# A two-layer convolution block: stores of the first layer on another queue, and another order of work at the edges of an image

## The chip, the cores and the metric

The kernel runs on one core of a Trainium2 chip. The metric is the device time of one execution in microseconds (us); for the kernel before it is 3935.01 us, the median of three runs (3934.5 to 3936.88). A core has five engines that run side by side, each taking its own instructions in order: TensorE (PE; its weight loads are shown as PEld), VectorE (DVE), ScalarE (ACT), GpSimd (POOL) and SyncE (SP), which here only issues DMA transfers.

## The reference, cut to what matters

x is 8 images of 256 channels and 64 x 64 pixels, in float32. Two residual layers follow one another:

```python
x = x + L0_conv_ref(gn(x), ...)
x = x + L1_conv_ref(gn(x), ...)

# layer 0 (per image): a 3x3 kernel made for every pixel and every group of 8 channels
x1, x2, x3 = conv1x1(x, w1, b1), conv1x1(x, w2, b2), conv1x1(x, w3, b3)
h = relu(bn(concat(x1, unfold3(reflect_pad(x2)))))       # 320 channels
w = conv1x1(relu(bn(conv1x1(h, cw1))), cw2, cb2)          # 9 weights for each of 32 groups
out = einsum('bgskhw,bgkhw->bgshw', unfold3(zero_pad(x3)), w)

# layer 1 (per image): 7x7 local attention (4 heads of 64) and a mix of depthwise convolutions
q, k, v = c1x1(x, Wq, bq) / 8, c1x1(x, Wk, bk), c1x1(x, Wv, bv)
att = softmax(einsum('bdn,bdkn->bnk', q, unfold7(reflect_pad(k)) + unfold7(reflect_pad(pe))))
out_att = einsum('bnk,bdkn->bdn', att, unfold7(reflect_pad(v)))
wts = softmax over 9 branches of einsum('oc,bchw->bohw', Wfc, x)
out_conv = sum over branches of wts * dwconv(relu(dwconv(x, w1)), w2)
out = rate1 * out_att + rate2 * out_conv
```

gn is a group norm with 32 groups, over whole images: layer 1 of an image can't start before layer 0 of that image is done.

## The kernel before, in words

An image is cut into NB = 8 bands of 8 rows (512 pixels); B * NB = 64 bands in all. One loop, `for g in range(-AHEAD, B * NB)` with AHEAD = 12 (L1030), makes layer 1 of band g and, beside it, layer 0 of a band some 12 further on. So in the first 12 turns (g < 0, called `alone`) only layer 0 runs; in the last 12 only layer 1. Every turn has STEPS = 8 steps, s = 0 to 7. The order of instructions on each engine is the order in which the program emits them; nothing reorders them.

Within a step there are fixed slots: `steer(g, s)` first (loads), then layer 1's scores and exponentials, a first `branch_weights` (L868), the functions in the list `mid`, a second `branch_weights`, and last the functions in the list `end`. `beside(g, s)` (L913) fills `mid` and `end`. A counter of places, `advance()`, moves on six times in a step; `after(n, f)` emits f n places later. A turn thus has 48 places: steer of step s is at place 6s, mid at 6s + 2, end at 6s + 5.

**Layer 0 of a band.** `load_x` (L99) brings x by channel (xc for the maps, xs for the statistics of a later image). `small_maps` (L328) makes x1 and x2. `value_maps` (L362) makes x3 in two halves: PE products L369, ScalarE adds the bias into x3n (L374), and SyncE stores x3n to DRAM (L375). In the alone turns this is in mid of steps 2 and 3, places 14 and 20. `x_by_group` (L399, steer of step 4) loads x again in another arrangement, xg: 32 groups x 4 quarters of the band on the 128 partitions, 8 channels x 128 pixels each; four DMAs (L405) of 128 KB, in pieces of 512 bytes. `values_by_group` (L381, step 5) loads x3 from DRAM in the same arrangement (x3q; L389, L393, L397: five DMAs, the last from the next band). `hidden_maps` (L409) has ScalarE make hid(0), hid(1), hid(2) (L420), PE convolve them (L430), and ScalarE write h2n (L437). `tap_weights` (L459) multiplies: PE makes weights pw (L466) from h2n, VectorE multiplies them with x3q into prod (L479), and POOL adds prod into xg (L487). In alone turns there are three groups of three taps; the third product of each goes to PE, which sums in PSUM (`gather`, L500), and VectorE adds that sum into xg (`combine`, L507, place 14 of the next turn). The products of a band are at places

```python
TAPS_AT = (1, 2, 3, 4, 5), (0, 2, 4)
PRODUCTS_AT = ((1, 2),) * 5, ((7, 14, 10), (9, 17, 13), (12, 20, 16))
```

(right-hand sets for alone turns: 12, 19, 15, then 26, 34, 30, then 41, 49, 45; the last of each three goes to PE). Prod has two buffers, so a product waits for the add before last. `take` (L509), one place after the sum, has VectorE make statistics (L515) and SyncE store xg to DRAM as x1 (L519, four DMAs). From turn -1 on the band's nine products all go to POOL.

**Layer 1 of a band.** `load_rows` (L547) loads a band of x1 with three rows on both sides into yp, `normalise` (L559) applies the group norm on ScalarE (L562). `values` (L575) makes v in two halves of two PSUM tiles (PE L592, ScalarE copies L600 into vc, one buffer), `store_values` (L607) writes vc to DRAM with its mirrored columns (L616; then L621, or L625 where the two halves of a row pair hold different numbers of rows), `mirror_rows` (L632) the mirrored rows, and `value_tile` loads the attention's tiles vt (L643). `position` (L650) makes the position map on POOL, `queries` (L661) makes qb (PE pq, ScalarE) and allots kb, with a POOL copy of the last rows of the band before; `keys` (L680) makes kb (PE pk, VectorE L700 and L707, and at the edges mirrored rows on ScalarE, L717). Scores (L736) read qb and kb, masks and maxima are on VectorE (L750), exponentials on ScalarE (L758, L767), transposes on PE (L773), weighted values on PE (L785). `branch_weights` is PE pf (L872) and ScalarE ex (L877). The PSUM tag "gen" (four buffers) holds pf, ptp, pq, pk, pv, pw and p3 in turn.

Edge bands are the first and last of an image. Their key products have other sizes (11 new rows for the first, 5 for the last, 8 inside), and in the last band of an image the next image's first two bands are loaded and two chunks of its values made. In the kernel before, `beside` puts for edge bands: queries of the second channel half at step 1 and its keys at step 2, queries and keys of the next band at steps 5 and 6; for inner bands these are steps 2, 3, 6 and 7. The last, keys of an inner band at step 7, are emitted ahead of `branch_weights` (L1055 to L1059).

Of the kernel before, what the change touches and what calls it, by code (L numbers as in the profile page):

```python
# [18 lines left out]
P = 128  # L19
# [4 lines left out]
R = 8  # L24
# [62 lines left out]
def conv_layers_kernel(ctx: ExitStack, tc: tile.TileContext, ins: dict, out: bass.AP):  # L87
# [271 lines left out]
        if i == NB - 1:  # L359
            nc.gpsimd.tensor_copy(t[0:96, R + 1, :], t[0:96, R - 1, :])  # L360

    def value_maps(b, i, mt):  # L362

        im = images[b]
        if mt == 0:
            im.x3[i] = dram.tile([C, R, HP], F32, tag="x3", name=f"x3_{b}_{i}")
        p3 = ps.tile([P, BAND], F32, tag="gen", name=f"p3_{b}_{i}_{mt}", bufs=4)
        for kt in range(NCT):
            nc.tensor.matmul(  # L369
                p3, im.w3s[:, kt, mt * P : (mt + 1) * P], im.xc[i][:, kt, :],  # L370
                start=(kt == 0), stop=(kt == NCT - 1),
            )
        p3 = p3.rearrange("p (r c) -> p r c", r=R)
        nc.scalar.activation(x3n[mt][:, :, 1 : 1 + W], p3, AF.Identity, bias=im.bias[:, 1 + mt : 2 + mt])  # L374
        nc.sync.dma_start(out=im.x3[i][mt * P : (mt + 1) * P], in_=x3n[mt])  # L375

    def pieces(v, q):

# [20 lines left out]
    def x_by_group(b, i, alone):  # L399

        tag, pool = ("ex", w1) if alone else ("xg", w0)
        t = pool.tile([P, SHARE, SR, W], F32, tag=tag, name=f"xg_{b}_{i}", bufs=3 if alone else 2)
        images[b].xg[i] = t
        for q in range(NQR):
            nc.sync.dma_start(  # L405
                out=t[q * REL : (q + 1) * REL].rearrange("p s r c -> p s (r c)"), in_=pieces(x_in[b][:, i * BAND : (i + 1) * BAND], q)
            )

    def hidden_maps(b, i, alone):  # L409

# [48 lines left out]
    def tap_weights(b, i, u, alone, at):  # L459
# [49 lines left out]
        def take():  # L509
            x = im.xg[i]  # L510
            if i == 0:
                im.st1 = stat.tile([P, 2 * NB, 6], F32, tag="st1", name=f"st1_{b}")
            for t in range(2):
                v = x[:, t * SHARE // 2 : (t + 1) * SHARE // 2].rearrange("p s r c -> p (s r c)")
                nc.vector.bn_stats(im.st1[:, 2 * i + t, :], v)  # L515
            t = im.x1[i] = dram.tile([C, BAND], F32, tag="x1", name=f"x1_{b}_{i}")
            for q in range(NQR):
                v = x[q * REL : (q + 1) * REL].rearrange("p s r c -> p s (r c)")
                nc.sync.dma_start(out=pieces(t, q), in_=v)  # L519

        for j in range(n):
            after(at[j], lambda j=j: product(j))
# [46 lines left out]

    def value_rows(j):  # L570

        first, last = (PAD, R) if j == 0 else (0, R) if j < NB else (R - 1, R + PAD)
        return first, last, first if j < NB else 0

    def values(b, j, half):  # L575

        im = images[b]
        if half == 0:  # L580
            im.vc[j] = w1.tile([P, R // 2, C], F32, tag="vc", name=f"vc_{b}_{j}", bufs=1)
        vc, yp = im.vc[j], im.yp[min(j, NB - 1)]
        first, last, _ = value_rows(j)
        pv = ps.tile([P, 2, C], F32, tag="gen", name=f"pv_{b}_{j}_{half}", bufs=4)
        done = []
        for g in range(2):
            r = first + 4 * half + 2 * g
            n = min(2, last - r) * W
            if n <= 0:
                break  # L590
            for kt in range(NCT):
                nc.tensor.matmul(  # L592
                    pv[:n, g], yp[:, kt, r : r + n // W].rearrange("p r c -> p (r c)"), wv[:, kt],
                    start=(kt == 0), stop=(kt == NCT - 1),
                )
            done.append(n)

        def take():
            if len(set(done)) == 1:
                nc.scalar.copy(vc[: done[0], 2 * half : 2 * half + len(done)], pv[: done[0], : len(done)])  # L600
            else:
                for g, n in enumerate(done):
                    nc.scalar.copy(vc[:n, 2 * half + g], pv[:n, g])

        return take

    def store_values(b, j):  # L607

        im = images[b]
        vc = im.vc[j]  # L610
        vd = im.vd[j] = dram.tile([R, WP, C], F32, tag="v", name=f"vd_{b}_{j}")
        first, last, at = value_rows(j)
        count = [(last - first + 1 - p) // 2 for p in range(2)]
        for p in range(2):
            to = vd[at + p : at + p + 2 * count[p] - 1 : 2, PAD : PAD + W]
            nc.sync.dma_start(out=to.rearrange("u c n -> c u n"), in_=vc[p * W : (p + 1) * W, : count[p]])  # L616
        for d in range(1, PAD + 1):
            for to, c in ((PAD - d, d), (PAD + W - 1 + d, W - 1 - d)):
                if count[0] == count[1]:
                    o = vd[at : at + 2 * count[0], to].rearrange("(u p) n -> p u n", p=2)  # L620
                    nc.sync.dma_start(out=o, in_=vc[c : c + W + 1 : W, : count[0]])  # L621
                else:
                    for p in range(2):
                        o = vd[at + p : at + p + 2 * count[p] - 1 : 2, to : to + 1].rearrange("u c n -> c u n")
                        nc.sync.dma_start(out=o, in_=vc[p * W + c : p * W + c + 1, : count[p]])  # L625

    def mirror_rows(b, j):

# [21 lines left out]
    def position(b, i):  # L650
# [7 lines left out]
            perow[:, a : a + n].unsqueeze(2).to_broadcast([P, n, W]),  # L658
        )

    def queries(b, i, ct):  # L661

        im = images[b]
        nm = f"{b}_{i}_{ct}"
        kb = im.kb[i, ct] = w1.tile([P, KW, WP], F32, tag="kb", name=f"kb_{nm}", bufs=3)
        if i:
            nc.gpsimd.tensor_copy(kb[:, : 2 * PAD], im.kb[i - 1, ct][:, R:])
        qb = im.qb[i, ct] = w1.tile([P, NT, TQ, TQ], F32, tag="qb", name=f"qb_{nm}")
        pq = ps.tile([P, R, W], F32, tag="gen", name=f"pq_{nm}", bufs=4)
        for kt in range(NCT):  # L670
# [9 lines left out]
    def keys(b, i, ct):  # L680


        im = images[b]
        first, last = new_keys(i)
        kb, pe = im.kb[i, ct], im.pe[i]
        bk = chan[:, ct, CBK : CBK + 1]
        pieces = []
# [225 lines left out]
    def beside(g, s):  # L913

        b, i = divmod(g, NB)
        bn, inx = divmod(g + 1, NB)
        mid, end = [], []

        early = i in (0, NB - 1)
        if g >= 0:  # L920
            if s == 2 - early:
                mid.append(lambda: queries(b, i, 1))
            if s == 3 - early:
                mid.append(lambda: keys(b, i, 1))
        early = inx in (0, NB - 1)
        if 0 <= g + 1 < B * NB:
            if s == 5 - early:
                mid.append(lambda: position(bn, inx))
            if s == 6 - early:
                mid.append(lambda: queries(bn, inx, 0))  # L930
            if s == 6 and early:
                mid.append(lambda: keys(bn, inx, 0))

        made = [(b, i + 2, 4)] if g >= 0 and i < NB - 1 else []
        if i == NB - 1 and 0 <= b + 1 < B:
            made = [(b + 1, 0, 3), (b + 1, 1, 5)]
        for bb, j, d in made:
            if s in (d, d + 1) and (j < NB or s == d):
                mid.append(lambda bb=bb, j=j, d=d: values(bb, j, s - d))
            if s == d + 1:  # L940
                end.append(lambda bb=bb, j=j: store_values(bb, j))
            if s == d + 2 and j in (0, NB):
                end.append(lambda bb=bb, j=j: mirror_rows(bb, j))
            if s == 7 and j != 1:
                for u in range(NT // 2):
                    end.append(lambda bb=bb, j=j, u=u: value_tile(bb, j, u))
# [3 lines left out]

        nxt = [(b, i + 2, 0)] if g >= 0 and i + 2 < NB else []
        if i == NB - 1 and 0 <= b + 1 < B:
            nxt = [(b + 1, 0, 0), (b + 1, 1, 1)]
        for bb, ii, d in nxt:
            if s == d:
                end.append(lambda bb=bb, ii=ii: load_rows(bb, ii))
# [4 lines left out]
        if 0 <= g + AHEAD < B * NB:  # L961
            bq_, iq = divmod(g + AHEAD, NB)
            if alone and s == 0:
                mid.append(lambda: small_maps(bq_, iq, small_tile(f"{bq_}_{iq}"))())
            if s == (2 if alone else 0):
                (mid if alone else end).append(lambda: value_maps(bq_, iq, 0))
            if s == (3 if alone else 1):
                mid.append(lambda: value_maps(bq_, iq, 1))
        if 0 <= g + AHEAD - 1 < B * NB and s == (2 if alone else 1):
            bh, ih = divmod(g + AHEAD - 1, NB)  # L970

# [6 lines left out]
        if 0 <= g + AHEAD - 2 < B * NB and s in TAPS_AT[g < -1]:  # L978
# [1 line left out]
            end.append(  # L980
                lambda: tap_weights(*divmod(g + AHEAD - 2, NB), u, g < -1, PRODUCTS_AT[g < -1][u])
            )
        return mid, end

    def steer(g, s):

# [21 lines left out]
    with tc.manual_schedule():  # L1008
# [21 lines left out]
        for g in range(-AHEAD, B * NB):  # L1030
            b, i = divmod(g, NB)
            for s in range(STEPS):
                ct, m = divmod(s, NT // 2)
                mid, end = beside(g, s)
                steer(g, s)
                if g >= 0:
                    nm = f"{b}_{i}_{ct}_{m}"
# [14 lines left out]
                    for a, po in weighted:  # L1052
                        add_values(*a, po)
                    tot = exponentials(nm, prob, nmax)
                ahead = s == 7 and 0 <= g + 1 < B * NB and (g + 1) % NB not in (0, NB - 1)  # L1055
                finish = keys(*divmod(g + 1, NB), 0) if ahead else None
                advance()
                if ahead:
                    finish()  # L1059
                if g >= 0:  # L1060
                    ex, exb = w1.tile([P, 2, BAND], F32, tag="ex", name=f"ex_{nm}", bufs=3), ex if m else None
                    branch_weights(b, i, ct, m, 0, ex)
# [44 lines left out]
def _layout(inputs):  # L1107

    a = {k.replace("L0_conv_", "a_").replace("L1_conv_", "b_"): np.asarray(v) for k, v in inputs.items()}
    f = np.float32  # L1110
    arr = {"x": a["x"].reshape(a["x"].shape[0], C, HW)}
    arr["w12"] = np.concatenate([a["a_w2"].T, a["a_w1"].T], axis=1)
    arr["w3"] = a["a_w3"].T

# [72 lines left out]
```

## Time and profile before

| | before |
|---|---|
| median of 3 runs | 3935.01 us (3934.5 to 3936.88) |
| the profiled execution, its own time | 3936.72 us |
| its span in the trace | 3934.9 us |
| busy PE, DVE, ACT, POOL | 3793.0, 3420.8, 2832.9, 3175.0 us |
| granted TensorE clock, mean | 0.992 |
| DMA: bytes, mean rate | 472.80 MB, 120 GB/s |
| first scores of layer 1 (L736) | 251.05 us |
| sum L507 of bands 0 to 8 | 72.07 to 227.10 us |
| DVE waits for x3q at the start | 8.60 us, to 54.89 us |

How to read it: the profile gives, for each engine, its instructions with start, duration and line of the kernel; in brackets stands how long the engine stood idle before an instruction and which instruction released it. The engine names SPq and ACTq stand for DMA issues by SyncE and ScalarE; their duration is that of the issue, not of the transfer. "x4" behind a line means that many instructions, merged. The windows of the profile give for each stretch of time the busy time of each engine, the granted clock of TensorE, the busy share of the 16 DMA engines and the rate in GB/s.

### The profile page before, as it was taken

Reading aid. Unit: us, or ns where it says so; the run is one execution under the profiler, and the core shown is the slowest. Engines: PE = TensorE matmul, PEld = TensorE weight load, DVE = VectorE, ACT = ScalarE, POOL = GpSimd, SP = SyncE. Lnnn points to the kernel's source line nnn. Section 1 sums busy time; section 2 is a strip of 40 time slices with the busy share of each in tenths; the row PEclk is TensorE's granted clock in tenths of the full one; section 3 lists DMA queues with packets and bytes.
Section 4 is the critical chain, followed back from the end, with each engine's and each line's share of the span. In section 5 each row is a group of like instructions: output and inputs, shape, how many; then the busy total and the mean of one; then the engine's idle time right before and its main releaser. Section 6 shows DMA issues by size and latency. Waiting matters only on the chain.

```text
span 3934.9 us, 71885 instructions
## 1 busy us (share of the span) xinstructions
PE 3793.0 (96%) x24620; PEld 2108.2 (54%) x24620; DVE 3420.8 (87%) x7143; ACT 2832.9 (72%) x6779; POOL 3175.0 (81%) x2156
## 2 busy tenths in 40 slices
PE   5789999999999999999999999999999999999998
PEld 2345555555555555555555555555555555555554
DVE  5769988898988998888998998989988889978778
ACT  3457777777777777777777777777777777677776
POOL 3758988888987988978887888978988888966665
PEclk9989999999999999999999999999999999999999
DMA  7874444544445444454444544454444543322211
GB/s 223 200 186 116 123 120 116 134 127 123 120 111 143 123 124 109 122 142 125 122 117 126 131 126 119 114 140 123 119 117 102 125 122 100 86 74 88 71 60 35
DMA packets 489711, 472.80 MB, mean 120 GB/s; under 512 B 64208, under 2 KB 390400, under 8 KB 489088
## 3 DMA queue, kind: packets, MB, share of 16 engines
q1 hardware_dynamic: 486016, 463.66, 44.5%
q8 instruction: 194, 3.18, 0.4%
q10 hardware_dynamic: 3328, 4.55, 0.3%
q14 instruction: 173, 1.42, 0.1%
HBM read 329.08 MB, written 142.43 MB: 120 GB/s over the span
## 4 chain that ended last, share of the span: by engine, by line
PE 43%; DVE 19%; POOL 17%; ACT 10%; issue 5%; DMA 3%; SPq 2%; POOLq 0%; DVEq 0%; ACTq 0%
PE pf L872 20%; POOL xg L487 8%; DVE prod L479 5%; POOL ex L1085 4%; DVE acc L855 4%; PE small L785 4%; DVE rec L893 4%; PE sco L736 3%; PE pv L592 3%; PE ptp L773 3%; ACT x L343 3%; PE pk L692 3%; PE pq L671 3%; ACT ex L877 2%; DVE acc L829 1%
## 5 line engine op out<-in xcount | busy, mean ns | idle before, releaser
L872 PE MATMUL pf<-yp,c_wfc 128*128 128x512 f32 x4096 | 1917.3, 595 | 19.2 <-ACT ex L877 16.9
L487 POOL TENSOR_TENSOR xg<-xg,prod 128x1024 f32<-128x1024 f32 x549 | 1200.6, 2187 | 144.8 <-DVE prod L479 105.0
L872 PEld LDWEIGHTS pf<-yp,c_wfc 128*128 128x128 f32 x4096 | 736.2, 190 | 721.7 <-issue 630.0
L1085 POOL TENSOR_TENSOR ex<-ex,ex 128x1024 f32<-128x1024 f32 x384 | 907.9, 2364 | 52.7 <-ACT ex L877 48.5
L479 DVE SCALAR_TENSOR_TENSOR prod<-pw,c_par,x3q 128x1040 f32<-128x1040 f32 x576 | 737.5, 1287 | 139.0 <-PE pw L466 67.6
L829 DVE SCALAR_TENSOR_TENSOR acc<-yp,c_chan,acc 128x504 f32<-128x504 f32 (+3 forms) x1104 | 775.0, 702 | 50.2 <-ACT acc L820 29.8
L855 DVE SCALAR_TENSOR_TENSOR acc<-hid,c_chan,acc 128x504 f32<-128x504 f32 (+3 forms) x1024 | 750.2, 733 | 20.0 <-ACT acc L849 1.9
L877 ACT ACTIVATE ex<-pf 128x512 f32<-128x512 f32 x1024 | 601.8, 588 | 202.4 <-PE pf L872 186.6
L758 ACT ACTIVATE prob<-prob,nmax 128x196 f32<-128x196 f32 x1024 | 459.2, 451 | 213.6 <-DVE nmax L750 213.3
L767 ACT ACTIVATE prob<-prob,tot 128x196 f32<-128x196 f32 x1024 | 413.1, 453 | 257.8 <-DVE tot L765 256.8
L894 POOL TENSOR_TENSOR tot<-tot,rec 128x256 f32<-128x256 f32 x254 | 185.2, 729 | 398.7 <-DVE rec L893 376.8
L893 DVE RECIPROCAL rec<-tot 128x256 f32<-128x256 f32 x256 | 445.8, 1741 | 10.6 <-POOL tot L888 4.9
L775 ACT COPY pt<-ptp 112x512 f32<-112x512 f32 x511 | 294.8, 577 | 101.0 <-PE ptp L773 100.4
L750 DVE CUSTOM_DVE_ANT_0 prob<-sco,c_mask 128x196 f32<-128x196 f32 x1024 | 324.2, 354 | 28.9 <-PE sco L736 28.6
L773 PEld LDWEIGHTS ptp<-ident,prob 128*112 128x112 f32 x2044 | 226.4, 133 | 188.6 <-issue 152.1
L773 PE MATMUL ptp<-ident,prob 128*112 128x128 f32 x2044 | 320.2, 279 | 1.3 <-ACT vc L600 1.3
L785 PEld LDWEIGHTS small<-pt,vt 112*64 112x64 f32 x8144 | 258.6, 138 | 77.5 <-issue 76.3
L785 PE MATMUL small<-pt,vt 112*64 112x64 f32 x8144 | 294.7, 225 | 0.4
L592 PE MATMUL pv<-c_wv,yp 128*128 128x256 f32 (+1 forms) x1056 | 253.8, 383 | 7.4 <-ACT yp L562 6.2
L369 PE MATMUL p<-xc,w3s 128*128 128x512 f32 x512 | 248.7, 609 | 8.7 <-ACT ex L877 8.7
L466 PEld LDWEIGHTS pw<-h2n,c_c 128*128 128x128 f32 x1152 | 175.5, 193 | 144.7 <-issue 116.5
L888 POOL TENSOR_SCALAR tot<-tot 128x512 f32<-128x512 f32 x127 | 243.6, 1918 | 11.1
(139 smaller groups left out, 4750.9 us busy)
## 6 DMA issues: line engine op xcount, KB each, us to landing
vt<-vd SPq DMA_DIRECT2D x512, 112.0 KB
x<-x3n SPq DMA_DIRECT2D x128, 264.0 KB
x3q<-x SPq DMA_DIRECT2D x128, 264.0 KB
xc<-in_x SPq DMA_DIRECT2D x64, 512.0 KB
xg<-in_x SPq DMA_DIRECT2D x256, 128.0 KB
x<-xg SPq DMA_DIRECT2D x256, 128.0 KB
yp<-x SPq DMA_DIRECT2D x128, 256.0 KB
xr<-x SPq DMA_DIRECT2D x64, 512.0 KB
```

Of the source, the lines that this page charges most:

```text
L479: nc.vector.scalar_tensor_tensor(prod[:, :, :RUN], pw[:, j, :RUN].unsqueeze(1).to_broadcast([P, SHARE, RUN]), par[:, PCB2 + k : PCB2 + k + 1],
L487: nc.gpsimd.tensor_add(im.xg[i], im.xg[i], rows(prod))
L758: nc.scalar.activation(prob[:, h, :NKEY], prob[:, h, :NKEY], AF.Exp, bias=nmax[:, h : h + 1], scale=-1.0, accum_out=tot[:, h : h + 1],)
L767: nc.scalar.activation(prob[:, h, :NKEY], prob[:, h, :NKEY], AF.Copy, scale=tot[:, h : h + 1])
L773: nc.tensor.transpose(ptp[:, h, ch], prob[:, h, ch * CHUNK : (ch + 1) * CHUNK], ident)
L785: nc.tensor.matmul(po[half[h], :, t * TQ : (t + 1) * TQ], im.vt[i + ch, m][:n, t, (2 * ct + h) * HD : (2 * ct + h + 1) * HD], pt[:n, h, ch ...
L829: nc.vector.scalar_tensor_tensor(o, yp[:, ct, ra + dr : rb + dr, ca + dc : cb + dc], chan[:, ct, CW1 + k : CW1 + k + 1], o, ALU.mult, ALU.add,
L855: nc.vector.scalar_tensor_tensor(o, hid[:, ra + dr : rb + dr, ca + dc : cb + dc], chan[:, ct, CW2 + k : CW2 + k + 1], o, ALU.mult, ALU.add,)
L872: nc.tensor.matmul(pf, wfc[:, kt, 2 * m + j, ct * P : (ct + 1) * P], images[b].yp[i][:, kt, PAD : PAD + R], start=(kt == 0), stop=(kt == N ...
L877: nc.scalar.activation(ex[:, j].rearrange("p (r c) -> p r c", r=R), pf, AF.Exp)
L893: nc.vector.reciprocal(rec, v)
L1085: after(4, lambda ex=ex, exb=exb: nc.gpsimd.tensor_add(ex, ex, exb))
```

## The change

1. In layer 0 alone (g < 0), the stores of x3n are issued by ScalarE, in `value_maps`. The stores of x1 by alone bands are moved out of `take` into `keep`, nine places later (place 24 of the turn), and issued by ScalarE; other bands' stay on SyncE and where they were.
2. The host adds x a second time in the arrangement of xg; `x_by_group` is one DMA of contiguous 4 KB rows, for all bands.
3. `value_rows` of an image's first chunk has six rows (rows 3 to 8) in place of five, so that all its PSUM tiles are full, `values` loses its case for partial tiles, and `store_values` the case with two DMAs for a mirrored column (L625): two and six DMAs in place of two and twelve.
4. At edge bands keys come before queries: keys at steps 2 and 6 in mid, queries at steps 3 and 7 in a new list `head`, ahead of `branch_weights`. kb is allotted by whichever comes first (`key_block`).
5. In an image's last band, the second chunk of the next image's values is made at steps 5 and 7 (before 5 and 6) and stored at the end of 7 (before 6); its rows are loaded at step 2 (before 1) and normalised at the ends of 3 and 4 (before 2 and 3).

```diff
-    def value_maps(b, i, mt):
+    def value_maps(b, i, mt, alone):
...
-        nc.sync.dma_start(out=im.x3[i][mt * P : (mt + 1) * P], in_=x3n[mt])
+        queue = nc.scalar if alone else nc.sync
+        queue.dma_start(out=im.x3[i][mt * P : (mt + 1) * P], in_=x3n[mt])
...
-        for q in range(NQR):
-            nc.sync.dma_start(
-                out=t[q * REL : (q + 1) * REL].rearrange("p s r c -> p s (r c)"), in_=pieces(x_in[b][:, i * BAND : (i + 1) * BAND], q)
-            )
+        nc.sync.dma_start(out=t.rearrange("p s r c -> p (s r c)"), in_=ins["xg"][b, i])
...
-            t = im.x1[i] = dram.tile([C, BAND], F32, tag="x1", name=f"x1_{b}_{i}")
+            im.x1[i] = dram.tile([C, BAND], F32, tag="x1", name=f"x1_{b}_{i}")
+            if alone:
+                after(9, lambda: keep(nc.scalar))
+            else:
+                keep(nc.sync)
+
+        def keep(queue):
             for q in range(NQR):
-                v = x[q * REL : (q + 1) * REL].rearrange("p s r c -> p s (r c)")
-                nc.sync.dma_start(out=pieces(t, q), in_=v)
+                v = im.xg[i][q * REL : (q + 1) * REL].rearrange("p s r c -> p s (r c)")
+                queue.dma_start(out=pieces(im.x1[i], q), in_=v)
...
-        first, last = (PAD, R) if j == 0 else (0, R) if j < NB else (R - 1, R + PAD)
+        first, last = (PAD, R + 1) if j == 0 else (0, R) if j < NB else (R - 1, R + PAD)
...
-        count = [(last - first + 1 - p) // 2 for p in range(2)]
+        count = (last - first) // 2
...
-                if count[0] == count[1]:
-                    o = vd[at : at + 2 * count[0], to].rearrange("(u p) n -> p u n", p=2)
-                    nc.sync.dma_start(out=o, in_=vc[c : c + W + 1 : W, : count[0]])
-                else:
-                    for p in range(2):
-                        o = vd[at + p : at + p + 2 * count[p] - 1 : 2, to : to + 1].rearrange("u c n -> c u n")
-                        nc.sync.dma_start(out=o, in_=vc[p * W + c : p * W + c + 1, : count[p]])
+                o = vd[at : at + 2 * count, to].rearrange("(u p) n -> p u n", p=2)
+                nc.sync.dma_start(out=o, in_=vc[c : c + W + 1 : W, :count])
...
+    def key_block(b, i, ct):
+
+        im = images[b]
+        if (i, ct) not in im.kb:
+            kb = im.kb[i, ct] = w1.tile([P, KW, WP], F32, tag="kb", name=f"kb_{b}_{i}_{ct}", bufs=3)
+            if i:
+                nc.gpsimd.tensor_copy(kb[:, : 2 * PAD], im.kb[i - 1, ct][:, R:])
...
         early = i in (0, NB - 1)
         if g >= 0:
-            if s == 2 - early:
-                mid.append(lambda: queries(b, i, 1))
-            if s == 3 - early:
+            if s == 2:
+                mid.append(lambda: keys(b, i, 1) if early else queries(b, i, 1))
+            if s == 3 and early:
+                head.append(lambda: queries(b, i, 1))
+            if s == 3 and not early:
                 mid.append(lambda: keys(b, i, 1))
-        early = inx in (0, NB - 1)
+        edge = inx in (0, NB - 1)
         if 0 <= g + 1 < B * NB:
-            if s == 5 - early:
+            if s == 5 - edge:
                 mid.append(lambda: position(bn, inx))
-            if s == 6 - early:
-                mid.append(lambda: queries(bn, inx, 0))
-            if s == 6 and early:
-                mid.append(lambda: keys(bn, inx, 0))
-
-        made = [(b, i + 2, 4)] if g >= 0 and i < NB - 1 else []
+            if s == 6:
+                mid.append(lambda: keys(bn, inx, 0) if edge else queries(bn, inx, 0))
+            if s == 7:
+                head.append(lambda: queries(bn, inx, 0) if edge else keys(bn, inx, 0))
+
+        made = [(b, i + 2, (4, 5))] if g >= 0 and i < NB - 1 else []
         if i == NB - 1 and 0 <= b + 1 < B:
-            made = [(b + 1, 0, 3), (b + 1, 1, 5)]
+            made = [(b + 1, 0, (3, 4)), (b + 1, 1, (5, 7))]
...
         if i == NB - 1 and 0 <= b + 1 < B:
-            nxt = [(b + 1, 0, 0), (b + 1, 1, 1)]
+            nxt = [(b + 1, 0, 0), (b + 1, 1, 2)]
...
+    quarters = arr["x"].reshape(-1, REL, SHARE, NB, NQR, PIECE)
+    arr["xg"] = quarters.transpose(0, 3, 4, 1, 2, 5).reshape(-1, NB, P, SHARE * PIECE)
```

## The prediction, written before the change was run

> **What bounds the kernel now.** I read the slices of the span first, then windows, waits and timelines. The windows (busy us of PE, PEld, DVE, ACT, POOL, then PE clock, DMA share, GB/s) split the run in four:
>
> ```profile
> 60.00:222.00 162.00, 132.19 (x648) 65.40 (x646) 132.76 (x145) 68.51 (x128) 123.40 (x89) 0.91 0.81 189
> 222.00:300.00 78.00, 62.42 (x305) 33.76 (x305) 48.58 (x97) 42.30 (x93) 40.46 (x25) 0.89 0.68 174
> 300.00:3483.00 3183.00, 3132.45 (x20699) 1754.84 (x20699) 2855.48 (x6001) 2380.14 (x5714) 2730.39 (x1833) 1.00 0.46 121
> ```
>
> From 300 us on PE is busy 98.4%: layer 1 is PE-bound. In 60 to 222 us, layer 0 alone, nothing is full: PE 82%, DVE 82%, POOL 76%, DMA 81%. A loop of waits sets the pace there. SyncE's timeline shows one turn:
>
> ```profile
> 130.55 2.57 SPq L519 DMA_DIRECT2D x<-xg  x4
> 133.16 0.62 SPq L99 DMA_DIRECT2D xs<-in_x  x1
> 133.88 0.43 SPq L375 DMA_DIRECT2D x<-x3n  x1
> 134.36 2.71 SPq L405 DMA_DIRECT2D xg<-in_x  x4
> 137.11 0.61 SPq L389 DMA_DIRECT2D x3q<-x  x1
> ...
> 140.37 0.61 SPq L397 DMA_DIRECT2D x3q<-x  x1
> ```
>
> and VectorE's the rest of it:
>
> ```profile
> 129.31 1.22 DVE L507 TENSOR_TENSOR xg<-sco_sum,xg 128x1024 f32<-128x1024 f32 x1
> ...
> 146.39 1.30 DVE L479 SCALAR_TENSOR_TENSOR prod<-pw,c_par,x3q 128x1040 f32<-128x1040 f32 x1 [2.61 <-DMA x3q<-x]
> ...
> 148.11 1.16 DVE L507 TENSOR_TENSOR xg<-sco_sum,xg 128x1024 f32<-128x1024 f32 x1
> ```
>
> The x1 store (L519) waits for the sum L507; SyncE takes its queue in order, so the loads of the next band stand behind that store; their x3q is what the next band's first product waits for; and that product stands ahead of the next L507 on VectorE. One turn: sum 1.2, store issues 2.6, xs 0.7, x3 store 0.5, xg 2.7, four of five x3q issues 3.3, last x3q to product 6.0, product 1.2, small VectorE work 0.5 = 18.7 us (129.31 to 148.11 is 18.8).
>
> At the seam between images PE has short holes, and SyncE and ScalarE run late:
>
> ```profile
> 678.69 1.98 PE L671 MATMUL pq<-yp,c_wq 128*128 128x512 f32 x4 [1.27 <-ACT ex L877]
> 696.78 1.98 PE L872 MATMUL pf<-yp,c_wfc 128*128 128x512 f32 x4 [0.86 <-ACT ex L877]
> ```
> ```profile
> 707.47 7.87 SPq L625 DMA_DIRECT2D vd<-vc  x12
> ```
> ```profile
> 716.72 0.59 ACT L600 COPY vc<-pv 128x512 f32<-128x512 f32 x1 [3.45 <-DMA vd<-vc]
> ```
>
> **What the skill says.** The Trainium skill, "DMA: Bandwidth & Descriptors", section "Anatomy of one DMA": a DMA's semaphore wait happens on the issuing sequencer before dispatch. The trace agrees: over 60 to 222 us SyncE waits 47.8 us at L375 for ScalarE and 13.5 us at L519 for L507, everything behind held. Same page, "Issuing engines are not separate DMA queues": a second issuer saves only sequencer time. Here that is exactly the scarce thing (13 us of SyncE issues in one turn), while the transfers' share, 0.81, stays shared. "Perfetto Trace Analysis", "DMA Optimizations": small DMAs pay per transfer, larger ones amortize it; xg now moves 512-byte pieces. The trace shows only mixed rates: 397 GB/s at a full share for wide rows, 189 at 0.81 here.
>
> **The change, part by part.**
>
> *Stores of layer 0 alone on ScalarE.* SyncE's queue loses L375 and L519; nothing left there waits for L507. ScalarE gains per band 2 x 0.4 + 4 x 0.6 = 3.2 us of issues, taken from SyncE's rows; its own issues of weights took 0.34 to 0.50 each, so 2 to 3.2 is the span and I take the top. Cover: ScalarE is busy 68.5 of 162 us, 8 per band of 18.8, and stands 45.4 us in 9 waits (5 each) before hid L420 for PE; the x1 stores, delayed by nine places, fall right before that hid. Queued behind them is hid(2), for which PE's hidden convolution waits. But that convolution follows the gather of the new band's product, about 3.7 us of VectorE after L507, so a store waiting for L507 and its 2.4 us lie under it. The x3 stores come 3 us earlier than now (x3n done 131.06, store at 133.88), but each delays a hid by 0.4 us. Uncovered, this would cost up to 3.2 us a band.
>
> What is late next: VectorE and POOL. sum 1.25, statistics 1.2, product for PE 1.23, product for POOL 1.23, then POOL's five remaining adds, 11.2 in one piece at 134.40, and the next sum needs the last add. Together 16.1; I add 0.2 for hand-offs and take 16.3. VectorE's own work is 14.8 to 15.5 per band, PE's 15.2 at the granted 0.91: both fit below. One turn without the SyncE link is in the trace: band 0's first product starts at 54.89, band 1's at 70.12, 15.2 us, while later ones stand 18 to 21 apart. Sums L507 run from 72.07 to 227.10, 8 turns, 155 us. After: 8 x 16.3 = 130, plus 6 for layer 1's weight preparation (2.3) and two chains of image statistics: 136. **Gain 19 us**; bounds 8 (turn of 17.7) and 25 (turn of 15.5).
>
> *x in its second layout.* One xg issue of 0.6 in place of four of 2.7, for every band. What the wider pieces save of the transfers themselves no row shows alone; it lies between nothing and the four issues' 2.7 us a band, and I count nothing, since after the change no transfer is the link. In the alone stage it leaves SyncE freer; before the first band it is on the path (42.91 to 45.6, then x3q): **2 us**. The first x3 stores now share ScalarE's ring with 3.75 MB of weights issued at 25 to 28.3 us; DMA is full to 40 us, so x3n of band 1 could wait: bounds -2 and 4. In the main stage SyncE is off the path: zero, hidden by PE; also if that cover went, it is fewer issues.
>
> *Hand-over, 222 to 300 us.* PE waits 5.86 us at 228.07 for yp, loaded behind x3q on SyncE; first scores at 251.05 wait for a ScalarE that stood 7.39 us for vd stores (L625, 12 issues, now 6 by the extra row: 7.9 to 3.9 us). POOL does all nine adds of band 9 itself: from its last add of band 8 (221.6) to first scores 29.4 us now. After: seven adds 15.7, copies 0.8, pe 1.4, gaps 1, last product and keys 3.2, reflect 0.9 = 23.0; I take 24. Gain 5.4. Then xs, today issued at 260.85 behind L616 and L621 of the second chunk, comes ahead of them since that chunk is stored a step later; VectorE waits 8.25 us for it and PE 3.24 after it. Together **9 us**, bounds 4 and 12.
>
> *Edge bands.* Same products, same evacuations. The 64-row chunk becomes 128 rows: PE time per row is equal (1.08 us for four there, 1.89 for eight full ones), ScalarE copies 0.2 us more, 8 times: nothing. Moved: queries from step 1 (beside value maps) to the head of step 3; from 5 to the head of 7; the second chunk's second half from 6, where keys already take two of the four PSUM buffers, to 7; its rows from 1 to 2, normalised in 3 and 4. The position map and the POOL copy of old keys move no earlier than a step ahead of the scores, as in inner bands. From 285 us on PE waits 30 us for pq, pf, pw and ptp, nearly all at seven seams: 4.3 each. The 1.27 at pq goes (step 1 becomes an inner band's, 0.2); ScalarE's 3.45 goes with six issues fewer; the ones at steps 3 and 6 go in part. I take half, **15 us**. Against it: the second chunk's eight stores (5.2 us) now lie at the end of step 7, before the twelve vt loads (8.7) and band 2's rows; those rows come 1 us later than now (743.8 against 742.9). If that shows on PE it is 7 x 1. Bounds -5 and 25.
>
> **Sum.** 19 + 2 + 9 + 15 = 45 us. The profiled execution took 3936.7 us (span 3934.9), 1.7 above the median of the runs shown: 3936.7 - 45 = 3891.7, and on the median's scale 3890.
>
> **Rivals.** (a) *Layer 0 gains, edges don't:* holes move to step 3 or 7 as ScalarE's backlog of 5 us at pf is unchanged. For: ScalarE's work per seam is the same; against: the pieces are spread. 3890 + 15 = 3905. (b) *DMA takes SyncE's place:* share 0.81 at 18.8 us is 15.2 us of transfers a band; x1 stores keep 512-byte pieces, and if bursts hold x3q the turn is 17.7: gain 8, hand-over 4, edges 12: 3911. Against: x3q can be issued some 6 us ahead of need. (c) *Everything gives:* turn 15.5, edges 25: 3872. (d) *Slower:* ScalarE becomes the link. Its stores hold the line hid, convolution, h2n, pw, product; if the 3.2 us add to a turn of 18.8 for 10 bands, +32, and early stores wait 2 behind the weights, less edges 15: 3935 + 19 = 3954. It decides once issues and their waits exceed the 5 us of ScalarE's idling before hid. Against: the order of work above.
>
> **Chances.** Forecast (3878 to 3898) 0.52; (a) 0.18; (b) 0.14; (c) 0.11; (d) 0.05. Faster by over 0.2% (7.9 us, about what measurement can tell from no change): 0.94; same 0.02, the tail of (b); slower 0.04. Range 3868 to 3915: it takes in (a), (b) and (c) and leaves out (d).
>
> **What would show it.** L507 every 16 to 16.5 us, POOL near 88% and DMA waits for x3q gone; no SyncE wait for L507; first scores near 225 us; L625 absent and no ScalarE wait for vd; pq at the head of steps without a hole. Wrong if L507 keeps 18 us or more, if ScalarE's hid grows late, or if pf or the first vt use waits at seams.

## The result and the profile after

The changed kernel takes 3909.43 us (median of 5 runs, 3904.32 to 3917.44) against 3934.5 us before (5 runs, 3932.43 to 3936.88): ratio 0.9938, 95% interval [0.9923, 0.9952], 25 us faster. Forecast were 3890 us and a gain of 45; the time lies in the range of 3868 to 3915, near the cases (a) and (b), not in the forecast's own 3878 to 3898. The profiled execution took 3911.49 us (span 3909.7). A second set of five on another chip gave 3912.61 (0.9945 [0.9931, 0.9958]); its profile has a span of 3907.2.

Four blocks of the span carry the whole comparison. Their borders are read off two timelines: VectorE's sums (L507 before, L505 after; the first and the ninth) and PE's scores L736 (the first of all, and the first of the second band of layer 1).

| block, us of the span | before | after | gain | predicted |
|---|---|---|---|---|
| start to the first sum | 72.1 | 68.9 | 3.2 | 2 |
| eight turns of layer 0 alone | 155.0 | 144.8 | 10.2 | 19 |
| ninth sum to the second band's scores (hand-over) | 91.7 | 86.0 | 5.6 | 9 |
| from there to the end (seams) | 3616.1 | 3610.0 | 6.1 | 15 |
| span | 3934.9 | 3909.7 | 25.2 | 45 |

Each block is read from one trace of each kernel. How far such readings spread, the later runs show where their program is the same: the first sum comes at 66.2 to 70.1 us with both layer-0 parts and at 69.6 and 72.1 with neither; the hand-over takes 85.2 to 87.9 us with all edge parts and the stores on ScalarE; an image of layer 1 differs by 0.3 us. So the start's 3.2 us is hardly told from spread; the other three gains are.

Two of the windows after (columns as in the windows of before; the first ends here at the ninth sum, at 222 us there):

```profile
60.00:213.70 153.70, 126.68 (x612) 63.37 (x608) 132.94 (x147) 68.78 (x128) 119.09 (x90) 0.92 0.78 216
300.00:3483.00 3183.00, 3132.16 (x20755) 1763.84 (x20748) 2852.35 (x6007) 2389.53 (x5734) 2727.18 (x1831) 1.00 0.43 120
```

VectorE's busy share rises from 82% to 86%; in the second window PE's 98.4% stays. SyncE's timeline of one turn after:

```profile
118.30 0.37 SPq L99 DMA_DIRECT2D xs<-in_x  x1
118.85 0.34 SPq L405 DMA_DIRECT2D xg<-in_xg  x1
119.24 0.56 SPq L390 DMA_DIRECT2D x3q<-x  x1
119.84 0.61 SPq L394 DMA_DIRECT2D x3q<-x  x1
127.11 2.10 SPq L390 DMA_DIRECT2D x3q<-x  x3
129.31 0.55 SPq L398 DMA_DIRECT2D x3q<-x  x1
```

xg is one issue of 0.34 us, and no store is left. From 120.45 to 127.11 SyncE stands at its third x3q issue until the x3 store that ScalarE issued at 122.88 has landed; nothing in the queue waits for a sum any more, so the loop through SyncE is open. VectorE's sums now stand 16.36 us apart where nothing disturbs them (87.42, 103.78, 120.15), against 18.8 in the turn that the prediction showed. The prediction said 16.3. What sets them is what it named, POOL's five adds in one piece and the sum that waits for the last (POOL, then VectorE):

```profile
108.88 11.23 POOL L485 TENSOR_TENSOR xg<-xg,prod 128x1024 f32<-128x1024 f32 x5 [2.16 <-DVE prod L477]
```
```profile
120.15 1.22 DVE L505 TENSOR_TENSOR xg<-sco_sum,xg 128x1024 f32<-128x1024 f32 x1 [0.68 <-POOL xg L485]
```

But two of the eight turns take 22.1 and 20.5 us. VectorE and ScalarE in the first of these:

```profile
147.37 0.17 DVE L266 RECIPROCAL sc_a<-sc_a 128x2 f32<-128x2 f32 x1 [2.14 <-ACT sc_a L262]
...
151.29 0.16 DVE L312 TENSOR_TENSOR bias<-pb,c_par 128x1 f32<-128x1 f32 x1 [2.17 <-PE pb L304]
```
```profile
141.27 5.06 ACTq L523 DMA_DIRECT2D x<-xg  x4
146.43 0.81 ACT L418 ACTIVATE hid<-x,bn1b,bn1s 96x512 f32<-96x512 f32 x1 [5.61 <-DMA x<-xg]
147.15 0.19 ACT L262 ACTIVATE sc_a<-sc_a 128x2 f32<-128x2 f32 x1
```

The four x1 stores hold ScalarE for 5.06 us here (2.6 to 5.1 over the nine bands). hid(2) comes behind them, and behind hid(2) the square root of image 1's statistics, for which VectorE stands 2.14 us. The issues themselves are not slow: the 36 of the nine bands take 0.56 to 0.97 us each (557/622/972 below are the least, median and greatest in ns). Between the first of the group and the other three, ScalarE stands 2.2 us:

```profile
L523 ACTq DMA_DIRECT2D x<-xg x36: 557/622/972, 71.8 to 221.9; - x36
```
```profile
141.27 0.59 ACTq L523 DMA_DIRECT2D x<-xg  x1
```
```profile
144.09 2.23 ACTq L523 DMA_DIRECT2D x<-xg  x3
```

The semaphore records of the trace tell why: the second issue waits until 144.07, when the x3 store that ScalarE issued at 138.09 has landed. It needs none of that store's data. This program's DMAs, whichever engine issues them, share eight completion semaphores (330 or 329 DMAs on each), and these issues wait until the last DMA on their own semaphore has landed. In the waits of 60 to 260 us PE's wait for hid grows from 7.4 to 15.2 us.

At the seam PE's holes have moved. Its timeline of the seam that the prediction showed:

```profile
659.66 1.98 PE L369 MATMUL p<-xc,w3s 128*128 128x512 f32 x4 [0.43 <-ACT ex L877]
...
676.15 1.99 PE L594 MATMUL pv<-c_wv,yp 128*128 128x256 f32 x8 [0.99 <-ACT qb L674]
...
697.95 1.98 PE L872 MATMUL pf<-yp,c_wfc 128*128 128x512 f32 x4 [1.11 <-DVE prod L477]
```

The 1.27 us at pq are gone, and 0.99 at pv and 1.11 at pf stand in their place. Summed over 300 to 3483 us, PE's holes at pf, p, pq, pv, pw, ptp and sco are 43 us before and 43 after.

### The profile page after: what moved, and what is told of

It reads as the page before. It is cut to its first block, busy times and chain, and to the rows that moved or that the text cites. A ratio compares the mean times of both kernels' runs of the same rounds, so it can differ in the third digit from the quotient of the medians.

```text
span 3909.7 us, 71679 instructions
## 1 busy us (share of the span) xinstructions
PE 3778.1 (97%) x24620; PEld 2112.2 (54%) x24620; DVE 3419.7 (87%) x7143; ACT 2835.8 (73%) x6779; POOL 3172.5 (81%) x2156
## 4 chain that ended last, share of the span: by engine, by line
PE 41%; DVE 24%; POOL 15%; ACT 11%; issue 6%; DMA 3%; SPq 0%; ACTq 0%; POOLq 0%; DVEq 0%
PE pf L872 19%; POOL xg L485 8%; DVE prod L477 7%; DVE acc L855 5%; DVE rec L893 5%; POOL ex L1087 4%; PE small L785 3%; PE pv L594 3%; ACT x L343 3%; PE ptp L773 3%; PE sco L736 3%; PE pk L692 2%; PE pq L670 2%; ACT ex L877 2%; DMA x<-x3n 2%
## 5 line engine op out<-in xcount | busy, mean ns | idle before, releaser
L855 DVE SCALAR_TENSOR_TENSOR acc<-hid,c_chan,acc 128x504 f32<-128x504 f32 (+3 forms) x1024 | 750.6, 733 | 18.1
L369 PE MATMUL p<-xc,w3s 128*128 128x512 f32 x512 | 248.3, 608 | 15.8 <-ACT ex L877 15.8
L594 PE MATMUL pv<-c_wv,yp 128*128 128x256 f32 x1056 | 252.1, 381 | 7.4 <-ACT qb L674 6.0
```

The lines of the kernel that those rows point to most:

```text
L855: nc.vector.scalar_tensor_tensor(o, hid[:, ra + dr : rb + dr, ca + dc : cb + dc], chan[:, ct, CW2 + k : CW2 + k + 1], o, ALU.mult, ALU.add,)
```

## The experiments

**Theories.** The one the result suggests: the layer-0 parts open the loop as predicted, but the x1 stores on ScalarE are not hidden; the edge parts move holes more than they close them. Rivals: transfers or the statistics themselves set the long turns; the halves need each other. All times beside the kernel before on the same chip (3934.55, 3934.92 and 3934.77 us in the three comparisons, four kernels each).

**1 and 2: each half alone.** The kernel before with L376's and L523's stores and the new xg, or with everything else of the diff.

> The kernel before with the two layer-0 parts alone (stores of layer 0 alone on ScalarE, x in its second layout). Theory: these parts give nearly all of what the trace shows ahead of the first scores, 16 of the 25 us, and nothing after the first turn: first scores at 235 to 237 us, layer-1 turns as before (57.6 inside, 60.4 to 63.5 at the edges), 3917 us. Rival: the two halves need each other (the hand-over gains only because six vd stores went with the edge parts): first scores at 240 or later and 3922 us or more.

> The kernel before with the edge parts alone (queries behind keys, second chunk and its rows later, seven rows in the first chunk). Theory: each seam gives about 1 us, the first turn 2 to 3, nothing ahead of the first scores but a shorter vd store: first scores at 248 to 251 us, 3926 us. Rival (the edge parts are worth the 15 us that were predicted and the layer-0 parts take some of that back): 3919 us or less, with a turn of the first band below 59 us.

Measured: 3918.78 us (0.9961 [0.9949, 0.9974]) and 3925.19 us (0.9975 [0.9967, 0.9984]). Both expectations hold (the second says seven rows; the kernel has six). The gains, 15.8 and 9.4, add up to that of the whole. Layer 0's parts have their first scores at 236.2 us and turns at the seam of 56.6, 63.5 and 61.0 us, those of before; the edge parts have 250.2, 57.9, 62.8 and 59.5. The halves don't need each other.

**3: the x1 stores later on ScalarE.**

```diff
-                after(9, lambda: keep(nc.scalar))
+                after(19, lambda: keep(nc.scalar))
```

> The changed kernel with the x1 stores of layer 0 alone delayed by 19 places and not nine, so that they are issued by ScalarE behind hid(2) and relu of the next band. Theory: the issues, 2.6 to 4.3 us for four, stand ahead of hid(2) in the changed kernel and cost 9 us before the first scores; behind it they cost less: the two turns with image statistics fall from 22.1 and 20.5 us to about 18, ScalarE's hid no longer waits for the store, first scores at 226 to 230 us, 3902 us. Rival (transfers set these turns, or the statistics themselves do): turns stay at 20 to 22, first scores at 234 to 236 us, 3909 us. Second rival: the issues land ahead of another small ScalarE step that PE needs, and the time rises.

Measured: 3908.14 us (0.9933 [0.9919, 0.9946]); from the changed kernel's 3909.43 the times alone can't tell it. The trace can: eight turns take 139.5 us and not 144.8, three of them 16.4; the long ones fall from 22.1 and 20.5 to 20.15 and 18.0; first scores come at 230.7; PE's wait for hid falls from 15.2 to 7.0 us. ScalarE's hid waits no longer for the store but for PE, and VectorE less for the root (ScalarE's timeline, then VectorE's):

```profile
144.13 0.81 ACT L418 ACTIVATE hid<-x,bn1b,bn1s 96x512 f32<-96x512 f32 x1 [5.59 <-PE ph L428]
```
```profile
145.07 0.17 DVE L266 RECIPROCAL sc_a<-sc_a 128x2 f32<-128x2 f32 x1 [1.64 <-ACT sc_a L262]
```

So the place of the stores costs 5.3 us of turns. Other traces agree: with the stores delayed by nine places on ScalarE the turns take 144.2 to 145.9 us (the changed kernel twice, runs 1 and 6), by nineteen 138.3 to 141.2 (runs 3 and 7 to 11). Two things change at once: hid(2) no longer stands behind the stores, and a group holds ScalarE for 2.6 to 3.6 us only. They weren't tried apart. The theory's 3902 us isn't reached.

The granted clock of TensorE has a share in the long turn, which the expectations left out. In the changed kernel it is 0.61 over 147 to 152 us, right after PE's wait for hid, and pb's matmuls take 2.40 us against 1.48 here. Run 7 has the same program as run 3 in this turn, no wait for the root, and 18.46 us at a clock of 0.91 where run 3 has 20.15 at 0.83 (run 7, then run 3, columns as before):

```profile
134.55:153.01 18.46, 16.09 (x89) 8.52 (x89) 16.32 (x27) 8.45 (x19) 13.76 (x10) 0.91 0.77 217
```
```profile
135.05:155.20 20.15, 17.35 (x88) 9.04 (x89) 16.39 (x26) 7.92 (x18) 14.08 (x12) 0.83 0.66 191
```

What lowers the clock isn't shown. The hand-over's 87.9 us against 86.0 lies within the spread.

**4: the x1 stores late on SyncE.** `after(19, lambda: keep(nc.sync))`.

> The changed kernel with the x1 stores of layer 0 alone back on SyncE, but 19 places later, behind the next band's x3q loads. Theory: not which engine issues decides but what stands behind the issue: SyncE has room, ScalarE is freed of 2.6 to 4.3 us a band, turns of 16.4 with and about 17 without statistics' cover, first scores at 226 to 230 us, 3902 us. Rival (SyncE's time and its order are the link again): turns back at 18 us or more, first scores at 245 to 251, 3920 us or more.

Measured: 3920.31 us (0.9965 [0.9953, 0.9978]), the rival's number; the theory's 3902 is refuted. Turns are 16.4 to 20.5, 146.6 in all, and the hand-over takes 92.6. SyncE's longest waits at loads (total, times and the longest in us):

```profile
SPq L99 <- DMA x<-x3n: 31.2, 5, 10.4
SPq L405 <- DMA x<-x3n: 12.6, 4, 4.3
```

These loads (xc and xs, xg) read nothing of x3; they wait for a completion semaphore, as above. Beside that, four stores stand for 3.3 us between x3q and the next loads (the four at 117.14, the next xc at 122.73). So it does matter which engine issues: run 3 has the same delay and 139.5 us. How much of the 7.1 us is the stores' place in SyncE's order, and how much which x3 store a load happens to wait for, isn't settled.

**5 and 6: the two layer-0 parts apart.** The kernel before with the new xg alone, and with the stores on ScalarE alone.

> The kernel before with x in its second layout alone: one xg issue a band in place of four, all stores on SyncE as before. Theory: the loop through SyncE is a sum of issues, and the four xg issues (2.7 us) stand in it as the x1 stores do; with one of 0.6 us the turn falls from 18.7 to 16.6 us, which is what the loop of POOL's adds allows anyway: sums every 16.4 to 17 us where no statistics stand, first scores at 233 to 238 us, 3918 us, nothing for layer 1. Rival (the stores alone open the loop, as the prediction had it, and the layout is worth 2 us at the start): turns stay at 18 to 18.8, first scores at 249, 3932 us.

> The kernel before with the stores of layer 0 alone on ScalarE, xg still in four issues. Theory: SyncE no longer waits for the sum, so its 2.7 us of xg issues have slack; turns 16.4 to 17.5 without statistics and 20 to 22 with, first scores at 237 to 240 us, 3921 us. Rival (SyncE's issues still set the turn, because xg and x3q together take 6 us behind the xs wait): turns of 18 or more, first scores at 247, 3930 us.

Measured: 3929.91 us (0.9988 [0.9981, 0.9994]) and 3934.11 us (0.9997 [0.9989, 1.0005]). The first fits neither theory nor rival (first scores at 243.3); in the second the turns are the theory's, first scores (246.1) and time nearly the rival's. By blocks: the layout alone takes 148.8 us for the turns (gain 6.2) and 70.7 to the first sum (1.4). The stores alone have turns of 145.5 (gain 9.5), nearly as good as both, but in this trace lose it at both ends: 74.1 us to the first sum (2 later than before), hand-over 94.4 (2.7 longer). In the layout alone a turn has still a wait for x3q:

```profile
116.18 0.55 SPq L397 DMA_DIRECT2D x3q<-x  x1
```
```profile
124.98 1.30 DVE L476 SCALAR_TENSOR_TENSOR prod<-pw,c_par,x3q 128x1040 f32<-128x1040 f32 x1 [3.02 <-DMA x3q<-x]
```

From the last x3q issue to the product are now 8.8 us, 6.0 in the turn of before that the prediction added up: in this turn the landing takes back what SyncE saves. With the stores alone xg's four issues hold SyncE for up to 4.6 us and more, though they themselves take 2.3 to 2.4: the rest are waits inside the group, at 111.34 for an xs load to land. Together the parts gain 10.8 in the turns; what the layout adds to the stores is mostly the two ends, 4.0 and 4.2 us. By the medians the two parts give 4.9 and 0.7 us alone and 15.8 together, so these two do need each other; of the 15 us between runs 6 and 1 the two traces, 9.8 apart in span, show only a part.

**7, 8 and 9: the edge parts one by one,** all with the later stores of run 3. The row alone has the old order of queries and keys and the old steps; the second run adds keys ahead of queries; the third has the row and the later chunk, but the old order. The steps' edit:

```diff
-            made = [(b + 1, 0, (3, 4)), (b + 1, 1, (5, 7))]
+            made = [(b + 1, 0, (3, 4)), (b + 1, 1, (5, 6))]
-            nxt = [(b + 1, 0, 0), (b + 1, 1, 2)]
+            nxt = [(b + 1, 0, 0), (b + 1, 1, 1)]
```

> The changed kernel with the later x1 stores (19 places), and of the edge parts only the sixth row of the first chunk of values (six stores in place of twelve); queries and keys, the second chunk and its rows are at the old steps. Theory: the row takes ScalarE's wait for vd away but no hole of PE; the seam's turns stay near those of before, 61 to 60.5 for band 0, 56.6 and 63.5 for bands 6 and 7: 3914 to 3916 us. Rival (the shorter vd store is the whole gain of the seam): turns as in the changed kernel, 59.5, 57.8, 62.8: 3908 us.

> The same with queries behind keys as in the changed kernel, while the second chunk and its rows stay at the old steps. Theory: the hole at pq (1.27 and 0.43 us) goes, and a part of it comes back one step later: band 0 59.7 to 60.5, band 7 62.8, band 6 57.8 (the position map and keys of the next band are what lengthens band 6): 3909 to 3912 us. Rival (the order of keys and queries moves holes about and gains nothing; the later chunk does): the turns of the kernel with the row alone.

> The same with the second chunk and its rows later as in the changed kernel, while queries and keys are in the old order. Theory: band 6 is back at 56.6 and band 7 loses the hole that step 6 has, but keeps the 1.27 at pq: band 7 62.8 to 63.5, band 0 59.5 to 60.5, so the seam is at least as good as in the changed kernel: 3908 to 3912 us. Rival: the later chunk brings nothing, and turns are those of the kernel with the row alone.

| edge parts in it | time, us | hand-over | bands 6, 7, 0 of later images | rest of the span |
|---|---|---|---|---|
| none (run 1, stores at nine places) | 3918.78 | 90.2 | 56.6, 63.5, 61.0 | 3617.3 |
| row | 3911.83 (0.9943 [0.9928, 0.9958]) | 85.4 | 56.6, 63.6, 61.0 | 3617.3 |
| row, keys first | 3907.24 (0.9928 [0.9913, 0.9943]) | 85.3 | 57.9, 62.8, 59.5 | 3611.5 |
| row, chunk later | 3915.96 (0.9949 [0.9933, 0.9966]) | 90.8 | 56.6, 63.6, 61.2 | 3618.6 |
| all three (run 3) | 3908.14 | 87.9 | 57.9, 62.8, 59.5 | 3611.4 |

The sixth row is worth about 5 us, once, in the hand-over, and nothing at a seam; runs without it have 90.2 to 94.4 us there, those with it 85.2 to 87.9, but for runs 4 and 9. Keys ahead of queries is the whole gain of the seams, 1.0 us at each (471.2 us an image against 472.2). The later chunk gains nothing at a seam. Its 5.4 us more in the hand-over stand in one trace, with the old order; with keys first, traces have 85.2 to 87.9 with the later chunk and 85.3 and 85.6 without, so no cost is shown. In the bands' turns the first two theories nearly hold, though both kernels are 2 us faster than they said; the third is refuted, and its rival holds.

**10: the square root ahead of hid(2).** In run 3, the second group mean of image 1 two places earlier: `after(3 if name == "a1" else 5, a3)`.

> The changed kernel with the later x1 stores, and in image 1's chain of statistics the second group mean two places earlier, so that its square root is issued by ScalarE ahead of hid(2) and not behind it. Theory: what is left of the long turn (20.15 us where 16.4 is undisturbed) is VectorE, which waits 1.64 us for that square root and 0.92 us for PE's pb: with the root ahead of hid(2) the turn falls to 18.5, first scores to 229, the time by 1.5 us. Rival (the chain's own VectorE work and PE's small matmuls fill the turn): 20 us and no change, or the wait moves to the group mean itself.

Measured: 3908.68 us (0.9933 [0.9918, 0.9948]); the long turn takes 21.9 us, not 18.5. PE's and VectorE's timelines:

```profile
140.46 0.56 PE L237 MATMUL pg_a<-d_a,c_gmat 128*128 128x2 f32 x2 [3.79 <-DVE d_a L250]
140.87 3.76 PE L369 MATMUL p<-xc,w3s 128*128 128x512 f32 x4
```
```profile
146.00 0.17 DVE L266 RECIPROCAL sc_a<-sc_a 128x2 f32<-128x2 f32 x1 [3.20 <-ACT sc_a L262]
```

The last rival: a tiny matmul (0.56 us) that waits 3.79 us for VectorE holds p behind it, p's evacuation stands ahead of the square root on ScalarE, and VectorE waits 3.20 where it waited 1.64. The turn's granted clock, 0.84, is that of run 3 (0.83), so it doesn't explain the 1.8 us.

**11 and 12: a better version, and the changed kernel beside it.** Run 8 (keys first, later stores, old steps of the chunk) with VectorE's two ends of the chain later:

```diff
-            after(4, a6)
+            after(8 if name == "a1" else 4, a6)
-            after(2, lambda: biases(pb))
+            after(6 if b == 1 else 2, lambda: biases(pb))
```

> The changed kernel with the later x1 stores and the second chunk at its old steps (as in the run keys_first), and image 1's chain of statistics spread: the reciprocal four places later and the three bias adds four places later, so that VectorE makes products where it now waits 1.64 us for the square root and 0.92 us for pb. Theory: the long turn falls from 20 us to 17.5, first scores to 229 us, 3904 us, and 5 us below the changed kernel in the same comparison. Rival (PE or POOL fills the turn, or the wait moves as it did with the earlier group mean): 20 us, 3907 us.

> The changed kernel once more, beside the others on one chip: 3909 us by its own runs (3904 to 3917).

Measured: 3903.42 us (3902.28 to 3907.25; 0.9926 [0.9914, 0.9939]) beside 3912.61 (3908.09 to 3913.26): 9 us below the changed kernel by the medians, no overlap, though the two profiled spans are only 2.0 apart (3905.2, 3907.2): the one profiled execution is among the slower of its five, the other among the faster. The spread chain itself isn't shown to gain: the long turn is 19.45 us at a clock of 0.82 (19.96 at 0.83 in run 8), and run 7 has 18.46 without it. The wait for the root is gone and the other is longer:

```profile
152.73 0.16 DVE L312 TENSOR_TENSOR bias<-pb,c_par 128x1 f32<-128x1 f32 x1 [1.47 <-PE pb L304]
```

and POOL waits 2.90 and 2.00 us for products in this turn. What the traces show over the changed kernel is the place of the stores (turns 139.1 against 145.9); hand-over (85.6, 85.2) and the rest (3611.0, 3609.9) gain nothing.

## Why the prediction was right and wrong

The time lies in the range given, but 25 us of 45 is not the forecast come true: the loop opened as described, three of the four terms gave about half of their size, and the sum landed between (a) and (b), which the range took in.

**Right.** The bound of layer 0 alone, SyncE's order, and its successor, POOL's chain of adds: 16.36 us undisturbed against 16.3. Inside its images layer 1 stays as it was (57.6 us for most bands). VectorE's 8.25 us for xs go, and ScalarE's 3.45 for vd at the seams, though these were worth nothing there (run 7: band 7 takes 63.6 us without them, 63.5 with); in the hand-over the wait for vd only falls from 7.39 to 4.54. From POOL's last add of band 8 (it ends at 212.2) to the first scores are 22.8 us, 23.0 by the sum of the prediction; that is in part luck, since with the later stores the same stretch takes 24.5 to 26.6. Of the signs it named, the sums at 16.4 us and the end of SyncE's wait for L507 came; POOL is at 77% and not 88 (119.09 of 153.7 us), first scores at 235.0 and not 225, and one sign of being wrong came too: ScalarE's hid grows late.

**Wrong: the stores are not hidden (turns, 19 given, 10.2 measured).** The failed step: "a store waiting for L507 and its 2.4 us lie under it", priced at nothing. The issues were sized rightly (2.4 to 2.7 us for four), but a group holds ScalarE for 2.6 to 5.1, since it also waits inside for earlier DMAs to land, and hid(2) stands right behind it. The cover was a mean, too: the 45.4 us before hid are waits of 1.95 to 9.72 us, four of the nine under 2.4. Moving the stores, run 3 gives 5.3 us of the missing 8.8. What the prediction drew from the Trainium skill, "DMA: Bandwidth & Descriptors", section "Anatomy of one DMA", for SyncE, that a DMA waits on its issuing sequencer, holds for ScalarE as well, and there compute stands behind it: the 2.2 us between the stores and the 5.61 us of hid above. This is the mechanism of rival (d), at a sixth of its price. The other 3.5 us: 6 us were given for statistics and weights; with the stores out of the way the eight turns exceed 8 x 16.36 = 130.9 by 8.6 (139.5). The weights take their 2.3 in the first turn (18.57); the turns with statistics exceed 16.36 by 3.8 and 1.7, more than was given. VectorE's stalls in the chain (1.64 and 0.92 us in run 3) stand in the first of these, and so does a lower granted clock: in run 7 the turn exceeds by 2.1 only. The shares of the two weren't tried apart.

**Wrong: the hand-over counts a stretch twice (9 given, 5.6 measured).** The prediction reckoned the turns from sum to sum, and the hand-over from POOL's last add. In the kernel before, 5.5 us lie between that add's end (221.6) and the ninth sum (227.10), for one reason:

```profile
224.68 2.51 DVE L479 SCALAR_TENSOR_TENSOR prod<-pw,c_par,x3q 128x1040 f32<-128x1040 f32 x2 [4.72 <-DMA x3q<-x]
```

The same x3q wait was taken off in the eighth turn and again as "gain 5.4". From the add to the first scores the gain is 6.6, but 4.0 of it lie ahead of the sum, in the eight turns. From sum to first scores the gain is 2.6 (24.0 to 21.3), with 3.0 more in the first band. Runs 1 and 7 show the sources: with the layer-0 parts alone the scores come 21.9 us after the sum already, and the first band's gain comes with the sixth row (64.4 us, 68.2 without), which has six vd stores fewer. At a seam they now take 3.22 us of SyncE, 7.87 before:

```profile
688.64 3.22 SPq L618 DMA_DIRECT2D vd<-vc  x6
```

The later chunk, which was to bring 3.5 here, brings nothing that the runs show.

**Wrong: edges (15 given, 6.1 measured).** The failed step: "the ones at steps 3 and 6 go in part. I take half". The holes were treated as closing where work leaves; they opened again where it went (0.99 us at pv behind qb in step 3, 1.11 at pf in step 6). This is rival (a)'s mechanism for the two parts that do nothing at the seam. Keys first is worth 1.0 us a seam. Why exactly that is not settled: PE's holes in the bands 6, 7 and 0 add up to 4.8 us before and 5.0 after at one seam, its busy time in them falls by 1.1 us (176.1 to 175.0), and no single row carries that.

**Start (2 given, 3.2 measured).** The size is not to be told: kernels with the new start have their first sum at 66.2 to 70.1 us, those with the old one at 69.6 (run 2) and 72.1. Stores on ScalarE without the layout have it at 74.1, so the fear of the weights ahead of the first x3 stores may have been right for that half; it was not tried apart.

**Rival (b)** holds in part: DMA's share stays high (0.81 to 0.78, so 15.7 to 14.1 us a turn of 19.4 and 18.1), and in run 5 a slower landing takes back what SyncE gives in the turn shown. In the changed kernel no product waits for x3q after the first, at 50.2 us.

## What to carry to other kernels

A DMA issue that moves to a compute engine is paid by what stands behind it there: place it behind the step others wait for, and price it with the waits that the issue itself has, for its data and for its completion semaphore. A merged row of issues hides such waits; look at the single ones. When a loop opens, stalls that were free inside it (statistics, tiny matmuls that wait for VectorE) come due, so list them with the new bound. Read the granted clock beside a turn's length before explaining it by the order of work. Cut a span into blocks with common borders before adding up gains, look how far the blocks of like programs spread, and credit a hole as closed only where the moved work meets an engine with room.

## What was not expected of the hardware

- Four x1 stores hold ScalarE 2.58 us in one band and 5.06 in another, while their issues take 2.4 to 2.7 in every band (2.4 on SyncE): the rest is waiting until an earlier DMA on the same completion semaphore has landed. This program uses eight such semaphores for all its DMAs.
- The same is so on SyncE: xg's four hold it for 2.71 us before and for 3.78 and 4.63 with the stores on ScalarE, with 2.3 to 2.6 us of issues in each.
- The same program took 18.46 us in one trace of the long turn and 20.15 in another, at granted clocks of 0.91 and 0.83.
